# An RWKV block's first tile: both output shares from one difference, value and receptance projected the other way round, the second key in halves, and a second norm that takes no mean of its own

## The chip, the core and the metric

The kernel runs on one core of one Trainium2 chip. The metric is the device time of one execution in microseconds. Engines are called TensorE (PE in the profile, PEld for its weight loads), VectorE (DVE), ScalarE (ACT), GpSimd (POOL) and SyncE (SP, which only issues transfers here).

## What is computed

x has 2 sequences of 4096 steps with 256 features. Two residual blocks follow each other, each on a layer norm of its input (with no learned scale). The attention block mixes each step with the one before it, projects key, value and receptance, runs a recurrence along time, and projects back:

```python
xk = x * time_mix_k + x_prev * (1.0 - time_mix_k)
...
k = jnp.einsum('btd,ed->bte', xk, W_k)
v = jnp.einsum('btd,ed->bte', xv, W_v)
r = jax.nn.sigmoid(jnp.einsum('btd,ed->bte', xr, W_r))
...
new_p = jnp.maximum(p, u + k_t)
scale_old = jnp.exp(jnp.maximum(p - new_p, NEG_CLAMP))
scale_cur = jnp.exp(jnp.maximum(u + k_t - new_p, NEG_CLAMP))
wkv_t = (scale_old * q + scale_cur * v_t) / (scale_old + scale_cur + EPS)
new_p2 = jnp.maximum(p + w, k_t)
scale_prev = jnp.exp(jnp.maximum(p + w - new_p2, NEG_CLAMP))
scale_new = jnp.exp(jnp.maximum(k_t - new_p2, NEG_CLAMP))
q2 = scale_prev * q + scale_new * v_t
...
y = r * wkv
return jnp.einsum('btd,ed->bte', y, W_o)
```

The feed-forward block has two gates of 1024 (one through silu), two layers of 1024 x 1024 with gelu, and a layer back to 256; its weights are ternary, with a scale for each output.

## The kernel before

Features lie on partitions (two chunks of 128, ND = 2), time along the free axis in tiles of 512 steps (TS), 16 tiles in all. A tile goes through norm, attention, second norm and feed-forward. The feed-forward is the bulk: each fp32 operand is split into a rounded part (hi) and a rest (lo), and every product is taken with both (split_product, L185 and L186). While the feed-forward of tile i runs, the generators attention(i + 1) and normalise(i + 2) are stepped between its blocks, so their work lies under its matmuls. The loop at the end of split_block sets that order.

The first tile has nothing to lie under. It is written out by hand in first_tile. Its helpers matmul, activation, add and on chain every instruction behind the last one of its engine, so each engine works in the order of the text; all of them are recorded at L357. The order is:

- norm of tile 0 in two halves of 256 steps (first_layernorm): mean by a matmul with a matrix of 1/256, subtraction on VectorE, squares on ScalarE, their sum over the two chunks on VectorE, variance by matmul (var), root, reciprocal, spread over the partitions by matmul (rstd), product on VectorE.
- projections (project). Two ways are in use. One scales the weights by the mix and by one minus the mix (scale) and takes four matmuls, two on xn and two on xn shifted by a step: key and value. The other mixes xn first (mx, then: two ScalarE passes and a GpSimd add per chunk) and takes two matmuls: receptance.
- differences(h), scales(h), state(h), result(h) for the two chunks h: a scan along time for the log-maximum (lm), the clamped differences (sc for the state, so for the output), exponentials and sigmoids, a scan for the numerator (num), and the output y. The log-maximum and numerator after the last step are copied on GpSimd into log_max and numer; the second tile copies them into its own scan states on VectorE (L251, L252).
- the output projection into four banks of half a tile (ps_o), added to x_sb, and a second first_layernorm on the sum, with matmuls for its mean; then the split into x_hi and x_lo, with which the feed-forward starts.

keep_warm issues matmuls whose result is not read. load_table makes ScalarE load an activation table early. A small partition_all_reduce on root calls that GpSimd operation once ahead of its use. normalise(1) (called second) is stepped once near the end of first_tile: it issues the load of tile 2 on GpSimd's queue, adds the two chunks of tile 1 on VectorE (both, L204), and sums that over the partitions on GpSimd (total, L206).

Loads: x of tile 0 comes in halves on SP and ACT, the attention weights on ACT (key), SP (value, receptance) and GpSimd's queue (output). GpSimd's queue also carries x of tile 1, and then w1, w2 and h1 of the feed-forward.

Of the kernel before, what the change touches and what calls it, by code (L numbers as in the profile page):

```python
# [14 lines left out]
P = 128  # L15
# [51 lines left out]
def split_block(ctx, tc, flags, x, vecs, w_attn, w1, w2, h1, h2, w3, out):  # L67
# [35 lines left out]
    for m, queue in enumerate((nc.scalar, nc.sync, nc.sync)):  # L103
        queue.dma_start(out=wa_sb[:, m], in_=w_attn[:, m])
# [33 lines left out]
    vector.tensor_scalar(unmix, vec[:, 0 : 3 * ND], -1.0, 1.0, ALU.mult, ALU.add)  # L138

# [61 lines left out]
    def total(a, b, tag):  # L201

        both = one.tile([P, TS], F32, tag=tag, name="both")
        marks["both"] = vector.tensor_tensor(both, a, b, ALU.add)  # L204
        everywhere = one.tile([P, TS], F32, tag="total", name="total")
        marks["sum"] = nc.gpsimd.partition_all_reduce(everywhere, both, channels=P, reduce_op=ReduceOp.add)  # L206
        return everywhere

    def layernorm(src, new_xc, tag, spread=False):


        mean = total(src[:, 0, :], src[:, 1, :], tag)
        if spread:
            yield
        xc = new_xc()
        for h in range(ND):
            vector.scalar_tensor_tensor(xc[:, h, :], mean, -1.0 / D, src[:, h, :], ALU.mult, ALU.add)
        if not spread:
            yield
        sq = wide.tile([P, ND, TS], F32, tag="wide", name="sq")  # L220
        scalar.activation(sq, xc, AF.Square)
        var = total(sq[:, 0, :], sq[:, 1, :], tag)
        if spread:
            yield
        rstd = one.tile([P, TS], F32, tag=tag, name="rstd")
        scalar.activation(rstd, var, AF.Sqrt, bias=eps, scale=1.0 / D)  # L226
        if not spread:
            yield
        for p in halves:
            vector.reciprocal(rstd[:, p], rstd[:, p])  # L230
            if spread and p is halves[0]:
                yield
        for h in range(ND):
            vector.tensor_tensor(xc[:, h, :], xc[:, h, :], rstd, ALU.mult)
        yield
# [50 lines left out]
    def normalise(i):  # L286

        x_sb = loaded.pop(i)
        if i + 1 < len(tiles):
            loaded[i + 1] = load_x(i + 1)  # L290
        xn = []

        def new_xn():

            xn.append(one.tile([P, ND, TS + 1], F32, tag="xn", name="xn"))
            if tiles[i][1] == 0:
                vector.memset(xn[0][:, :, 0:1], 0.0)
            else:
                vector.tensor_copy(xn[0][:, :, 0:1], prev)
            return xn[0][:, :, 1:]  # L300

        yield from layernorm(x_sb, new_xn, "rstd1", spread=True)
        vector.tensor_copy(prev, xn[0][:, :, TS:])
        normal[i] = (x_sb, xn[0])
# [74 lines left out]
    def first_layernorm(src, xc, means):  # L379
# [4 lines left out]
        for mean, p in zip(means, halves):  # L384
            for h in range(ND):
                add(xc[:, h, p], src[:, h, p], mean, ALU.subtract)
            activation(sq[:, :, p], xc[:, :, p], AF.Square)
        varis = []
        for p in halves:
            add(sq[:, 0, p], sq[:, 0, p], sq[:, 1, p])  # L390
            var = ps_ffn.tile([P, TS // 2 // P], F32, tag="pf", name="var")
            for b in range(TS // 2 // P):
                t = slice(p.start + b * P, p.start + (b + 1) * P)
                matmul(var[:, b : b + 1], sq[:, 0, t], mean_w[:, 0:1], start=True, stop=True)
            varis.append(var)
            yield
# [12 lines left out]
        for rstd, p in zip(spread, halves):  # L409
            for h in range(ND):  # L410
                add(xc[:, h, p], xc[:, h, p], rstd, ALU.mult)
            yield

    def first_tile(second):

        x_sb = loaded.pop(0)
        xn = wide.tile([P, ND, TS], F32, tag="wide", name="xn0")
# [23 lines left out]
        norm = first_layernorm(x_sb, xn, means)  # L441
# [3 lines left out]
        scaled = [[hid.tile([P, ND, D], F32, tag=tag, name="ws") for tag in ("hi", "lo")] for m in range(2)]  # L445
# [5 lines left out]

        next(norm)
# [8 lines left out]
        keep_warm(unread, 3, 2 * P)  # L461
        scale(0, (1, 1), (0, 1))
        scale(1, (0, 0), (1, 0), (1, 1), (0, 1))
# [4 lines left out]
        for c in range(ND):  # L468
            j = 2 * ND + c
            activation(mx[:, c, :], xn[:, c, :], AF.Copy, scale=vec[:, j : j + 1])  # L470
            activation(then[:, c, 1:], xn[:, c, : TS - 1], AF.Copy, scale=unmix[:, j : j + 1])
            on("gpsimd", "tensor_tensor", mx[:, c, 1:], mx[:, c, 1:], then[:, c, 1:], ALU.add)
# [4 lines left out]

        def project(m, h, kind, p=whole):
# [3 lines left out]
            if m == 2:  # L482
                for c in range(ND):
                    matmul(ps, wa_sb[:, 2, c, block], mx[:, c, :], start=c == 0, stop=c == ND - 1)
                return ps
            now, then = (ws[:, :, block] for ws in scaled[m])
            skip = 1 if p.start == 0 else 0
            shifted = slice(p.start + skip - 1, p.stop - 1)
            matmul(ps, now[:, 0, :], xn[:, 0, p], start=True, stop=False)
# [6 lines left out]
        keys = [[(project(0, 0, attn, p), p) for p in halves], [(project(0, 1, attn), whole)]]  # L496
# [3 lines left out]
        def differences(h):  # L500
            w, u = col(DECAY, h), col(FIRST, h)
            for k, p in keys[h]:
                t, after = lm[h][:, p], lm[h][:, p.start + 1 : p.stop + 1]
                on("vector", "tensor_tensor_scan", after, w.to_broadcast([P, p.stop - p.start]), k,
                   lm[h][:, p.start : p.start + 1], ALU.add, ALU.max)
                on("vector", "scalar_tensor_tensor", sc[h][1][:, p], t, w, k, ALU.add, ALU.subtract)
                on("vector", "scalar_tensor_tensor", so[h][1][:, p], k, u, t, ALU.add, ALU.subtract)
# [3 lines left out]
        def scales(h):  # L511
            activation(sc[h][0], sc[h][0], AF.Exp)
            activation(sc[h][1], sc[h][1], AF.Relu)
            activation(sc[h][1], sc[h][1], AF.Exp, scale=-1.0)


        def state(h):
            on("vector", "scalar_tensor_tensor", sc[h][1], sc[h][1], MIN_SCALE, v[h], ALU.max, ALU.mult)
            on("vector", "tensor_tensor_scan", num[h][:, 1:], sc[h][0], sc[h][1], num[h][:, 0:1], ALU.mult, ALU.add)
            on("gpsimd", "tensor_copy", numer[:, h : h + 1], num[h][:, TS:])  # L520

        def result(h):
            for share, of in zip(so[h], (num[h][:, 0:TS], v[h])):
                on("vector", "scalar_tensor_tensor", share, share, MIN_SHARE, of, ALU.max, ALU.mult)
            add(so[h][0], so[h][0], so[h][1])

        for h in range(ND):
            differences(h)
            scales(h)
            activation(so[h][0], so[h][1], AF.Sigmoid, scale=-1.0)  # L530
            activation(so[h][1], so[h][1], AF.Sigmoid)
# [4 lines left out]
        state(0)  # L536
        result(0)
        state(1)
        add(y[:, 0, :], so[0][0], r[0], ALU.mult)
        result(1)  # L540
        for p in halves:
            add(y[:, 1, p], so[1][0][:, p], r[1][:, p], ALU.mult)
        with behind("vector"), behind("scalar"):
            next(second)
        last["vector"] = marks["both"]
# [3 lines left out]
        ]  # L549
        for c in range(ND):  # L550
            for ps_of, p in zip(banks, halves):
                for h in range(ND):
                    matmul(ps_of[h], wa_sb[:, 3, c, h * P : (h + 1) * P], y[:, c, p], start=c == 0, stop=c == ND - 1)
        means = []
        for ps_of, p in zip(banks, halves):
            mean = ps_ffn.tile([P, TS // 2], F32, tag="pf", name="mean")
            for h in range(ND):
                add(x_sb[:, h, p], x_sb[:, h, p], ps_of[h])
                matmul(mean, mean_w, x_sb[:, h, p], start=h == 0, stop=h == ND - 1)
            means.append(mean)  # L560
        unread = ps_attn.tile([P, TS], F32, tag="pa", name="unread")
        keep_warm(unread, 4)
        x2 = wide.tile([P, ND, TS], F32, tag="wide", name="x2")
        x2_hi = one.tile([P, ND, TS], F32R, tag="x2_hi", name="x2_hi")
        x2_lo = one.tile([P, ND, TS], F32R, tag="x2_lo", name="x2_lo")
        norm = first_layernorm(x_sb, x2, means)
        for _ in range(4):
            next(norm)
        keep_warm(unread, 6)
        run(norm)  # L570
        for p in halves:
            activation(x2_hi[:, :, p], x2[:, :, p], AF.Copy)
            add(x2_lo[:, :, p], x2[:, :, p], x2_hi[:, :, p].bitcast(F32), ALU.subtract)
# [8 lines left out]
    def ffn(i, x1, x2):  # L582

        ha = []
        for f in range(NH):
            fs = slice(f * P, (f + 1) * P)
            pa = ps_ffn.tile([P, TS], F32, tag="pf", name="pa")
            split_product(pa, lambda c: w1_sb[:, c, fs], x2)
            pb = ps_ffn.tile([P, TS], F32, tag="pf", name="pb")
            split_product(pb, lambda c: w2_sb[:, c, fs], x2)  # L590
# [55 lines left out]
    second = normalise(1)  # L646
    first_tile(second)
# [309 lines left out]
```

## Time and profile before

| what | us |
|---|---|
| runs of the kernel before | 1547.36, 1547.98, 1548.09 (median 1547.98) |
| the profiled execution | 1547.97 |
| its span, first to last instruction | 1546.2 |
| TensorE busy in the span | 1535.7 |
| VectorE, ScalarE, GpSimd busy | 1069.9, 1048.7, 241.2 |
| first feed-forward matmul starts | 39.91 |

In lines of the timeline and of the chain the first number is the start in us after the span's start, the second the length. Behind an instruction stands what it writes and reads (out<-in), its shape, and in brackets how long its engine was idle ahead of it and what ended the wait. TensorE's busy time is modelled, so its share says little; the start of one matmul against the start of the one before it says more. A 128x512 matmul in plain fp32 shows as two passes.

### The profile page before, as it was taken

What the parts mean: (1) busy time and instruction counts of PE and PEld (TensorE: products, weight loads), DVE (VectorE), ACT (ScalarE), POOL (GpSimd) and SP (SyncE); (2) the same over time, 40 slices, a digit from 0 to 9 for tenths busy, and PEclk for the clock granted to TensorE, in tenths of its full rate; (3) what the DMA queues carried; (4) which work ended last, traced back from release to release, by engine and by line L of the source; (5) the groups of instructions that cost most, each with busy time, mean ns of one, the idle gap of its engine ahead of it and who ended that gap; (6) DMA issues with size and microseconds to landing.
All of it is one profiled execution on the core that took longest, in us unless ns stands there. A gap on an engine that the chain in (4) does not pass through costs nothing.

```text
span 1546.2 us, 16526 instructions
## 1 busy us (share of the span) xinstructions
PE 1535.7 (99%) x6260; PEld 1173.5 (76%) x6260; DVE 1069.9 (69%) x1598; ACT 1048.7 (68%) x1349; POOL 241.2 (16%) x118
## 2 busy tenths in 40 slices
PE   9999999999999999999999999999999999999998
PEld 6778777777877778777787777877777787777886
DVE  6887676867768667785777767677685777855531
ACT  6685957759487595866858668595775858656542
POOL 4122012110211102112011121101111021100100
PEclk9999999999999999999999999999999999999999
DMA  7612031220302104031130311203122030210302
GB/s 266 142 43 101 14 116 35 70 81 14 130 22 95 55 17 141 7 109 41 42 116 9 120 35 54 97 9 121 35 75 75 14 130 21 96 41 29 115 9 82
DMA packets 39702, 109.16 MB, mean 71 GB/s; under 512 B 3712, under 2 KB 12672, under 8 KB 39104
## 3 DMA queue, kind: packets, MB, share of 16 engines
q1 hardware_dynamic: 25760, 79.86, 15.9%
q0 software_dynamic: 13296, 27.53, 5.8%
q8 instruction: 51, 0.84, 0.2%
q10 hardware_dynamic: 560, 0.66, 0.1%
q14 instruction: 35, 0.29, 0.1%
HBM read 99.64 MB, written 12.58 MB: 73 GB/s over the span
## 4 chain that ended last, share of the span: by engine, by line
PE 97%; DVE 2%; ACT 1%; issue 0%; DVEq 0%
PE ph L185 30%; PE ph L186 30%; PE pa L185 4%; PE po L186 4%; PE po L185 4%; PE pb L185 4%; PE pa L186 4%; PE pb L186 4%; PE ps_r L178 3%; PE ps_v L178 3%; PE ps_k L178 3%; PE ps_o L178 3%; PE ps_k L357 0%; PE unread L357 0%; DVE scale L357 0%
## 5 line engine op out<-in xcount | busy, mean ns | idle before, releaser
L185 PE MATMUL ph<-hi,h_sb 128*128 128x512 f32 x2048 | 818.1, 400 | 0.2 <-ACT hi L192 0.2
L186 PE MATMUL ph<-lo,h_sb 128*128 128x512 f32 x2048 | 812.3, 398 | 0.0
L185 PEld LDWEIGHTS ph<-hi,h_sb 128*128 128x128 f32 x2048 | 384.6, 188 | 100.0 <-issue 17.4
L186 PEld LDWEIGHTS ph<-lo,h_sb 128*128 128x128 f32 x2048 | 384.5, 188 | 99.1 <-issue 15.6
L206 POOL PARTITION_ALL_REDUCE total<-both x60 | 204.5, 3408 | 865.2 <-DVE both L204 424.4
L611 DVE TENSOR_TENSOR lo<-full,hi 128x512 fp32r<-128x512 f32 x256 | 195.8, 768 | 140.7 <-ACT full L610 137.3
L608 ACT ACTIVATE hi<-ph,vec 128x512 fp32r<-128x512 f32 x256 | 175.5, 685 | 126.6 <-PE ph L186 125.6
L592 ACT ACTIVATE gated<-pa,vec 128x512 f32<-128x512 f32 x128 | 87.3, 682 | 140.2 <-PE pa L186 138.4
L610 ACT ACTIVATE full<-ph,vec 128x512 f32<-128x512 f32 x256 | 174.9, 683 | 0.2
L593 DVE SCALAR_TENSOR_TENSOR gated<-pb,vec,gated 128x512 f32<-128x512 f32 x128 | 95.8, 749 | 71.0 <-PE pb L186 66.5
L608 ACT ACT_TABLE_LOAD x104 | 133.4, 1283 | 1.8
L230 DVE RECIPROCAL rstd<-rstd 128x256 f32<-128x256 f32 x60 | 102.6, 1729 | 2.6 <-ACT rstd L226 2.6
L192 ACT ACTIVATE hi<-gated 128x512 fp32r<-128x512 f32 x128 | 80.6, 630 | 35.1 <-DVE gated L593 34.8
L185 PE MATMUL pb<-x_hi,w_sb 128*128 128x512 f32 x256 | 102.0, 398 | 0.6 <-ACT gated L592 0.6
L185 PE MATMUL pa<-x_hi,w_sb 128*128 128x512 f32 x256 | 101.9, 398 | 0.1
L186 PE MATMUL pb<-x_lo,w_sb 128*128 128x512 f32 x256 | 100.6, 393 | 0.0
L186 PE MATMUL pa<-x_lo,w_sb 128*128 128x512 f32 x256 | 100.5, 393 | 0.0
L193 DVE TENSOR_TENSOR lo<-gated,hi 128x512 fp32r<-128x512 f32 x128 | 96.3, 761 | 5.8 <-ACT hi L192 0.7
L186 PE MATMUL po<-lo,w_sb 128*128 128x512 f32 x256 | 100.2, 392 | 0.0
L185 PE MATMUL po<-hi,w_sb 128*128 128x512 f32 x256 | 100.2, 391 | 0.0
L617 DVE SCALAR_TENSOR_TENSOR x_sb<-po,vec,x_sb 128x512 f32<-128x512 f32 x32 | 24.0, 751 | 73.4 <-PE po L186 73.4
L261 DVE TENSOR_TENSOR_SCAN lm<-vec,lm,ps_k 128x512 f32<-128x512 f32 x30 | 38.4, 1279 | 41.3 <-PE ps_k L178 41.3
(145 smaller groups left out, 1745.2 us busy)
## 6 DMA issues: line engine op xcount, KB each, us to landing
h_sb<-h_hbm SPq DMA_DIRECT2D x128, 512.0 KB, 3.3
raw<-in_h SPq DMA_DIRECT2D x32, 256.0 KB, 2.7
x_sb<-in_x POOLq DMA_DIRECT2D x15, 512.0 KB, 4.0
out<-x_sb POOLq DMA_DIRECT2D x15, 512.0 KB, 3.1
h_sb<-in_h POOLq DMA_DIRECT2D x1, 4096.0 KB, 20.1
h_hbm<-in_h POOLq DMA_DIRECT2D x8, 512.0 KB, 8.9
w_sb<-in_w POOLq DMA_DIRECT2D x3, 1024.0 KB, 10.9
raw<-in_w SPq DMA_DIRECT2D x12, 256.0 KB, 2.6
```

The lines of the kernel that those rows point to most:

```text
L178: tensor.matmul(psum, weights(c), src[c], start=c == 0, stop=c == n - 1)
L185: tensor.matmul(psum, weights(c), hi, start=c == 0, stop=False)
L186: tensor.matmul(psum, weights(c), lo, start=False, stop=c == n - 1)
L192: marks["rounded"] = scalar.activation(hi, full, AF.Copy)
L193: marks["rest"] = vector.tensor_tensor(lo, full, hi.bitcast(F32), ALU.subtract)
L206: marks["sum"] = nc.gpsimd.partition_all_reduce(everywhere, both, channels=P, reduce_op=ReduceOp.add)
L230: vector.reciprocal(rstd[:, p], rstd[:, p])
L592: scalar.activation(full, pa, AF.Silu, scale=col(S1, f))
L593: vector.scalar_tensor_tensor(full, pb, col(S2, f), full, ALU.mult, ALU.mult)
L608: scalar.activation(hi, ps, AF.Gelu, scale=col(scales, f))
L610: marks["rounded"] = scalar.activation(full, ps, AF.Gelu, scale=col(scales, f))
L611: marks["rest"] = vector.tensor_tensor(lo, full, hi.bitcast(F32), ALU.subtract)
```

## The change

Everything is in the first tile and in the first block of its feed-forward.

- The output shares are no longer computed from a difference of their own. The difference for the state, p + w - k (sc[h][1]), plus or minus a constant per feature (offset, decay plus first), gives both sigmoids' arguments through the bias of the activation. One VectorE pass per half key goes, and sigmoids of both chunks follow each other (shares), after the exponentials of both.
- Value is projected from mixed inputs (mx), with 2 matmuls for each chunk; receptance from one chunk with scaled weights and one mixed chunk (mxr), with 3. The receptance weights are loaded ahead of the value weights.
- The key of the second chunk is projected and scanned in halves, as that of the first was.
- state(1) stands ahead of result(0).
- The second norm takes no mean: the output weights are centred (each row of them less its own mean over the outputs), the first norm's centred input xc is kept apart from xn (in the buffer of x2_lo), and xc plus the product with the centred weights is the centred sum. The product with the plain weights is computed too (gain, 4 matmuls of 512 columns) and added to x_sb later, for the residual. The variance matmuls sum over both chunks, and the VectorE sum of squares goes from the second norm (not from the first).
- The sum of the two chunks of tile 1 (both) moves from VectorE to GpSimd, near the start of first_tile.
- keep_warm in the second norm: 2 in place of 4, and gain[1] in place of 6. The split is taken chunk by chunk for the rest, and the first feed-forward block takes all products with the rounded part first.

```diff
-    for m, queue in enumerate((nc.scalar, nc.sync, nc.sync)):
+    for m, queue in ((0, nc.scalar), (2, nc.sync), (1, nc.sync)):
         queue.dma_start(out=wa_sb[:, m], in_=w_attn[:, m])
...
+    offset = const.tile([P, 2, ND], F32, name="offset")
+    vector.tensor_tensor(offset[:, 0, :], vec[:, DECAY : DECAY + ND], vec[:, FIRST : FIRST + ND], ALU.add)
+    vector.tensor_scalar(offset[:, 1, :], offset[:, 0, :], -1.0, None, ALU.mult)
...
-    def first_layernorm(src, xc, means):
+    def first_layernorm(xc, out, centre):
         sq = wide.tile([P, ND, TS], F32, tag="wide", name="sq")
-        for mean, p in zip(means, halves):
-            for h in range(ND):
-                add(xc[:, h, p], src[:, h, p], mean, ALU.subtract)
-            activation(sq[:, :, p], xc[:, :, p], AF.Square)
         varis = []
         for p in halves:
-            add(sq[:, 0, p], sq[:, 0, p], sq[:, 1, p])
+            centre(xc, sq, p)
+        yield
+        for p in halves:
             var = ps_ffn.tile([P, TS // 2 // P], F32, tag="pf", name="var")
+            chunks = range(1 if xc is not out else ND)
+            if xc is not out:
+                add(sq[:, 0, p], sq[:, 0, p], sq[:, 1, p])
             for b in range(TS // 2 // P):
                 t = slice(p.start + b * P, p.start + (b + 1) * P)
-                matmul(var[:, b : b + 1], sq[:, 0, t], mean_w[:, 0:1], start=True, stop=True)
+                for c in chunks:
+                    matmul(
+                        var[:, b : b + 1], sq[:, c, t], mean_w[:, 0:1], start=c == 0, stop=c == chunks[-1]
+                    )
...
+        with behind("vector"):
+            on("gpsimd", "tensor_tensor", summed, loaded[1][:, 0, :], loaded[1][:, 1, :], ALU.add)
         scale(0, (1, 1), (0, 1))
-        scale(1, (0, 0), (1, 0), (1, 1), (0, 1))
+        scale(2, (0, 1), (1, 1))
         run(norm)
         mx, then = (wide.tile([P, ND, TS], F32, tag="wide", name="mx") for _ in range(2))
-        for c in range(ND):
-            j = 2 * ND + c
-            activation(mx[:, c, :], xn[:, c, :], AF.Copy, scale=vec[:, j : j + 1])
-            activation(then[:, c, 1:], xn[:, c, : TS - 1], AF.Copy, scale=unmix[:, j : j + 1])
-            on("gpsimd", "tensor_tensor", mx[:, c, 1:], mx[:, c, 1:], then[:, c, 1:], ALU.add)
+        mxr, thenr = (hid.tile([P, TS], F32, tag=tag, name="mxr") for tag in ("hi", "lo"))
+        for m, c, mixed, step in ((1, 0, mx[:, 0, :], then[:, 0, :]), (1, 1, mx[:, 1, :], then[:, 1, :]), (2, 0, mxr, thenr)):
+            j = m * ND + c
+            activation(mixed, xn[:, c, :], AF.Copy, scale=vec[:, j : j + 1])
+            activation(step[:, 1:], xn[:, c, : TS - 1], AF.Copy, scale=unmix[:, j : j + 1])
+            on("gpsimd", "tensor_tensor", mixed[:, 1:], mixed[:, 1:], step[:, 1:], ALU.add)
...
+        centred = hid.tile([P, ND, D], F32, tag="hi", name="centred")
+        row = tmp.tile([P, ND], F32, tag="each", name="row")
+        for c in range(ND):
+            on("vector", "tensor_reduce", row[:, c : c + 1], wa_sb[:, 3, c, :], mybir.AxisListType.X, ALU.add)
+        on("vector", "tensor_scalar", row, row, 1.0 / D, None, ALU.mult)
+
+        def centre(c):
+            on("vector", "tensor_scalar", centred[:, c, :], wa_sb[:, 3, c, :], row[:, c : c + 1], None, ALU.subtract)
+
+        centre(0)
...
-            if m == 2:
+            if m == 1:
                 for c in range(ND):
-                    matmul(ps, wa_sb[:, 2, c, block], mx[:, c, :], start=c == 0, stop=c == ND - 1)
+                    matmul(ps, wa_sb[:, m, c, block], mx[:, c, :], start=c == 0, stop=c == ND - 1)
                 return ps
...
+            if m == 2:
+                matmul(ps, now[:, 1, :], xn[:, 1, :], start=True, stop=False)
+                matmul(ps[:, 1:], then[:, 1, :], xn[:, 1, shifted], start=False, stop=False)
+                matmul(ps, wa_sb[:, m, 0, block], mxr, start=False, stop=True)
+                return ps
...
-        keys = [[(project(0, 0, attn, p), p) for p in halves], [(project(0, 1, attn), whole)]]
+        keys = [[(project(0, h, attn, p), p) for p in halves] for h in range(ND)]
...
-                on("vector", "scalar_tensor_tensor", so[h][1][:, p], k, u, t, ALU.add, ALU.subtract)
...
         def scales(h):
+            activation(so[h][0], sc[h][1], AF.Relu)
+            activation(so[h][0], so[h][0], AF.Exp, scale=-1.0)
             activation(sc[h][0], sc[h][0], AF.Exp)
-            activation(sc[h][1], sc[h][1], AF.Relu)
-            activation(sc[h][1], sc[h][1], AF.Exp, scale=-1.0)
+        def shares(h):
+            activation(so[h][1], sc[h][1], AF.Sigmoid, bias=offset[:, 1, h : h + 1])
+            activation(sc[h][1], sc[h][1], AF.Sigmoid, bias=offset[:, 0, h : h + 1], scale=-1.0)
...
-        for h in range(ND):
-            differences(h)
-            scales(h)
-            activation(so[h][0], so[h][1], AF.Sigmoid, scale=-1.0)
-            activation(so[h][1], so[h][1], AF.Sigmoid)
+        differences(0)
+        scales(0)
+        differences(1, lambda: centre(1))
+        scales(1)
+        for h in range(ND):
+            shares(h)
...
         state(0)
+        state(1)
         result(0)
-        state(1)
...
+        gain = [ps_sum.tile([P, TS], F32, tag="ps", name="gain")]
+        def output(h, c):
+            matmul(gain[h], wa_sb[:, 3, c, h * P : (h + 1) * P], y[:, c, :], start=c == 0, stop=c == ND - 1)
         for c in range(ND):
             for ps_of, p in zip(banks, halves):
                 for h in range(ND):
-                    matmul(ps_of[h], wa_sb[:, 3, c, h * P : (h + 1) * P], y[:, c, p], start=c == 0, stop=c == ND - 1)
-        means = []
-        for ps_of, p in zip(banks, halves):
-            mean = ps_ffn.tile([P, TS // 2], F32, tag="pf", name="mean")
-            for h in range(ND):
-                add(x_sb[:, h, p], x_sb[:, h, p], ps_of[h])
-                matmul(mean, mean_w, x_sb[:, h, p], start=h == 0, stop=h == ND - 1)
-            means.append(mean)
-        unread = ps_attn.tile([P, TS], F32, tag="pa", name="unread")
-        keep_warm(unread, 4)
+                    matmul(ps_of[h], centred[:, c, h * P : (h + 1) * P], y[:, c, p], start=c == 0, stop=c == ND - 1)
+            output(0, c)
+        unread = ps_attn.tile([P, TS], F32, tag="pa", name="unread")
+        gain.append(ps_attn.tile([P, TS], F32, tag="pa", name="gain"))
+        keep_warm(unread, 2)
+        def plus_output(x2, sq, p):
+            for h in range(ND):
+                add(x2[:, h, p], xc[:, h, p], banks[p.start * 2 // TS][h])
+                activation(sq[:, h, p], x2[:, h, p], AF.Square)
...
-        keep_warm(unread, 6)
+        for c in range(ND):
+            output(1, c)
         run(norm)
...
+        for h in range(ND):
+            add(x_sb[:, h, :], x_sb[:, h, :], gain[h])
...
+            if i + f:
+                split_product(pa, lambda c: w1_sb[:, c, fs], x2)
+                split_product(pb, lambda c: w2_sb[:, c, fs], x2)
+            else:
+                for k in range(2):
+                    for ps, sb in ((pa, w1_sb), (pb, w2_sb)):
+                        for c in range(ND):
+                            tensor.matmul(
+                                ps, sb[:, c, fs], x2[c][k], start=k + c == 0, stop=k == 1 and c == ND - 1
+                            )
```

## The prediction

> **What bounds the kernel now.** I read the page first. The chain that ended last is TensorE for all but 3% of the span:
>
> ```profile
> span 1546.2 us, 16526 instructions
> ...
> PE 97%; DVE 2%; ACT 1%; issue 0%; DVEq 0%
> ```
>
> The tiles after the first keep TensorE fed and the change leaves their order as it was, so only the way to the first feed-forward matmul can move the time. That way is short. The chain of waits in order of time, cut to 10 to 42 us (start, length, what):
>
> ```profile
> 11.29 6.88 PE ps_k L357 x24
> 18.17 3.44 PE ps_v L357 x8
> ...
> 21.72 0.70 DVE scale L357
> ...
> 22.44 1.30 DVE state L357
> ...
> 28.35 1.21 DVE scale L357 x2
> ...
> 30.85 1.99 PE ps_o L357 x8
> 32.84 1.74 PE mean L357 x8
> ...
> 35.39 0.64 ACT sq L357
> ...
> 36.54 0.61 PE var L357 x4
> ...
> 39.91 0.50 PE pa L185
> ```
>
> Three stretches: TensorE projects until the first value is there (21.6), VectorE works without a gap from 21.72 to the first half of y[1] (30.38 + 0.42 = 30.80), and then projection, mean, norm and split run one after another until the feed-forward starts at **39.91**. Every microsecond off 39.91 is one off the end, as far as the backlog of the first feed-forward allows. The profiled execution took 1547.97 us with a span of 1546.2, so 1.8 lie around it; the median of the three runs is 1547.98, and I sum against 1547.97.
>
> Last I read the timeline of GpSimd, because the change gives it work (start, length, what, in brackets the idle time before):
>
> ```profile
> 16.03 0.20 POOL L357 COPY prev<-xn 128x2 f32<-128x2 f32 x1
> 23.93 0.86 POOL L357 PARTITION_ALL_REDUCE root<-eps  x1 [7.70 <-ACT scale L357]
> ...
> 27.95 0.90 POOL L96 DMA_DIRECT2D x_sb<-in_x  x1
> ...
> 31.83 3.26 POOL L206 PARTITION_ALL_REDUCE total<-both  x1 [2.12 <-DVE both L204]
> ...
> 49.31 3.23 POOL L206 PARTITION_ALL_REDUCE total<-both  x1 [8.59 <-DVE both L204]
> ```
>
> and beside the last of these VectorE:
>
> ```profile
> 49.03 0.74 DVE L593 SCALAR_TENSOR_TENSOR gated<-pb,vec,gated 128x512 f32<-128x512 f32 x1
> 49.86 2.22 DVE L193 TENSOR_TENSOR lo<-gated,hi 128x512 fp32r<-128x512 f32 x1
> ```
>
> Two facts. The first all-reduce (on root) comes 7.70 us after the copy of prev, though it needs only an activation that was done at 16.24: its first use costs 7.7. And a VectorE operation with two SBUF inputs that starts during an all-reduce ends 2.78 us after the all-reduce began (49.31 to 52.08; the next at 97.79 does the same to an add, 98.25 + 2.32 = 100.57). Operations with one input in PSUM pass: during the one at 31.83 the four adds of ps_o take 0.42 each as always.
>
> **Part by part.**
>
> *Projections.* A 128x512 matmul is two passes of 0.43 (24 passes of ps_k, half of them 256 wide, 11.13 to 18.0). Value goes from 8 matmuls to 4 (16 passes to 8), receptance from 4 to 6. The first value is ready at 18.0 + 4 x 0.43 + 0.16 = 19.9 instead of 21.6; receptance ends 4 passes, 1.7, earlier, at 26.8. The second key in halves costs no pass and gives its first scan at 16.5. ScalarE trades two weight scalings (0.40 apart) for two more mixings (0.61 apart): its last mixing starts at 14.5 instead of 14.0. The value weights now load behind the receptance weights (the two SP loads take 7.4 to landing, issued by 2.6): both are there by some 10.3, needed at 10.6 and 18. Nothing.
>
> *Shares from one difference.* One VectorE pass of 0.48 fewer for each half key (three passes, with the full one of 0.75), two table loads of 1.28 fewer on ScalarE, two one-input passes more. VectorE gets two row sums, a small scaling and a centring of 128x256 ahead of the first scan. None is in the trace; bounds from 0.17 (128x6) to 0.75 (scan of 256), I take 0.42 (a 128x256 add) and 0.30, in all 1.3 after xn ends at 11.73, so 13.0 against the key at 13.06: hidden; if it is 1.3 late, the gap before the second key (16.5) takes half of it. The differences end at 20.1. State(0) could start at 20.1, not 21.72: **-1.6, if nothing else is late.**
>
> *What is late next.* The second tile's sum (both) now runs on GpSimd early, so its all-reduce waits no longer for VectorE, and it starts as soon as GpSimd's queue lets it: mixings (three, 1.28 each, the last at 15.3), copy of prev at 16.5, 7.70 for the first use, 24.4; 0.74 later four copies at 0.125, done by 25.75; the load of tile 2 with 0.90, and the all-reduce at **26.6 to 29.9**, amid the y chain. Two prices. (a) VectorE's copies of log_max and numer into the next tile's state (L251, L252) stand in its order ahead of the add of result(0), and wait for GpSimd's copies until 25.7; VectorE comes there at 25.2. Behind them: add, y[0], result(1), y[1], and TensorE's ps_o. (b) Add 25.8 to 26.5, y[0] to 27.1, then share x numerator of h = 1, two SBUF inputs, meets the all-reduce: it ends at 26.6 + 2.78 = 29.4 instead of 27.8. Then 0.6 (share x v), 0.69 + 0.04 (add), y[1] first half 30.74 to **31.16**. Before: 30.80. The gain of the first stretch is gone: **+0.36**. Bounds for (b): 0 (all-reduce elsewhere) to 2.2.
>
> [...]
>
> *The sum on GpSimd itself.* Tile 1 lands at 1.30 + 6.6 = 7.9 (DMA view), so both (1.28, as the mixing of 511) runs at about 8.1 to 9.4, where VectorE adds the squares of the second half (8.37 to 8.79, two SBUF inputs). No row shows a GpSimd add against such an operation. Bounds: 0, or to the end of it, 9.4 + 0.42, which moves var from 9.09 to 9.88: +0.8 for all behind it. The nearest row is the all-reduce, which blocks for two thirds of its length: **+0.5**.
>
> *Second norm.* From y[1] on TensorE is a queue without holes: 8 passes ps_o 8 x 0.215 = 1.72, gain[0] 2 x 0.43 = 0.86, two warmers 2 x 0.235 = 0.47, a switch of 0.11, var of both chunks 16 x 0.115 = 1.84 (before: 4 loads in 0.52 for half of one half's work), rstd to the start of gain[1] 1.19, gain[1] 4 x 0.43 = 1.72: 7.9. Squares (ends 34.1), roots, products (end 38.4) and x_hi (second chunk 39.2) fit within it, the last just. Before it was 30.85 to 39.91 = 9.06; gone are mean (8 passes), subtraction (1.6) and sum of squares (0.43). **-1.1.** Gained outputs are added to x_sb by VectorE (2 x 0.68) before the first gated product is due: nothing, at most 0.7.
>
> *First feed-forward block.* pa is complete after its sixth matmul and not its eighth, some 0.25 sooner after the start. TensorE later idles there 1.2 us behind VectorE and ScalarE (pb at 51.69 to 52.92) and 0.8 at 61; I take **-0.25**, bounds 0 and -0.5.
>
> Sum: +0.36 + 0.5 - 1.1 - 0.25 = -0.5. **Forecast 1547.4.**
>
> **Rivals.**
>
> 1. *The all-reduce misses the y chain* (first use shorter or longer, so that the VectorE operations lie beside it in another order). Then y[1] follows VectorE alone: 29.2; TensorE is free at 26.9 + 1.72 + 0.86 = 29.5; feed-forward at 29.5 + 7.9 = 37.4, -2.5, and -0.25: **1545.2**. Against: 3.3 us of blocking in a chain of 9 us whose operations are two-SBUF for half of the time.
> 2. *Both blocks at full price* (+0.8 instead of +0.5, and no gain in the backlog): +0.36 + 0.8 - 1.1 = 0: **1548.0**. The change would do what it says and gain nothing.
> 3. *Slower: TensorE loses its rate.* The first matmuls of the program take 0.43 for 512 columns of the short kind (eight in 3.78), those of the feed-forward 0.23; the change drops six of ten warmers and leaves TensorE idle from 29.5 to 31.2. If that idle time lowers the rate, some 5 us (as at the start, 1.3 to 6.3) run at half: 5 x (1 - 0.23/0.43) = +2.3, **1549.7**. It decides if an idle of 1.7 us is enough; against it, after the idle 51.92 to 52.92 the next matmuls are 0.23 apart again.
>
> **How the numbers follow.** Forecast 0.50, rival 1 0.20, rival 2 0.19, rival 3 0.07, other 0.04 (half each way). The range leaves out most of rival 3 and the lower edge of rival 1: 1544.9 to 1549.0. A difference of 0.2%, 3.1 us, is about what a measurement of this kernel can tell from no change: faster means below 1544.9, a third of rival 1 and the odd case, 0.08; slower above 1551.1, 0.04; the rest, 0.88, is the same.
>
> **What would show it.** In the profile after: the all-reduce on total at 26 to 28, with a two-SBUF product or add of 2 us beside it; y[1] at 31 (rival 1: at 29.2); the add of squares at 8.4 stretched to 1 us or not; TensorE without a hole from y[1] to the feed-forward in 7.9 us; first pa at 39.2 to 39.7. Wrong would be: a first feed-forward before 38, or matmuls of the feed-forward 0.43 apart.

## The result, and the profile after

The changed kernel takes 1558.12 us (median of 6 runs, 1557.65 to 1558.96) against 1547.78 for the kernel before (median of 6, 1547.36 to 1548.09): 1.0067 times as long, interval 1.0057 to 1.0077. It is 10.3 us slower, and far outside the range. The profiled execution took 1557.65, with a span of 1555.9. The page of the kernel after, its span and its chain:

```profile
span 1555.9 us, 16540 instructions
...
PE 98%; DVE 1%; ACT 0%; issue 0%; POOL 0%; DVEq 0%
```

The chain is even more TensorE's than before (97%), so the time did not go into a new wait. The first tile went much as predicted. GpSimd's timeline of the kernel after:

```profile
8.78 1.32 POOL L362 TENSOR_TENSOR both<-x_sb 128x512 f32<-128x512 f32 x1 [3.81 <-DMA x_sb<-in_x]
...
24.95 0.40 POOL L362 PARTITION_ALL_REDUCE root<-eps  x1 [8.01 <-ACT scale L362]
...
26.68 3.20 POOL L211 PARTITION_ALL_REDUCE total<-both  x1
```

VectorE's timeline beside the last of these:

```profile
25.83 0.68 DVE L362 TENSOR_TENSOR scale<-scale 128x512 f32<-128x512 f32 x1
26.62 0.69 DVE L362 TENSOR_TENSOR y<-scale,ps_r 128x512 f32<-128x512 f32 x1
27.22 2.19 DVE L362 SCALAR_TENSOR_TENSOR scale<-scale,state 128x512 f32<-128x512 f32 x1
...
31.25 0.75 DVE L362 TENSOR_TENSOR y<-scale,ps_r 128x256 f32<-128x256 f32 x2 [0.52 <-DVE scale L362]
```

and TensorE's behind that:

```profile
31.73 1.99 PE L362 MATMUL ps_o<-y,centred 128*128 128x256 f32 x8 [1.51 <-DVE y L362]
...
37.82 1.88 PE L362 MATMUL gain<-y,wa_sb 128*128 128x512 f32 x4
39.14 1.03 PE L650 MATMUL pa<-x_hi,w_sb 128*128 128x512 f32 x2
```

The all-reduce falls into the chain to y[1] (26.68), a product with two SBUF inputs beside it takes 2.19, and the first feed-forward matmul still starts 0.77 sooner than before. What happens to that lead, from the starts of the first matmuls of each stage in both traces:

| start of | before | after | difference |
|---|---|---|---|
| first feed-forward matmul | 39.91 | 39.14 | -0.77 |
| its first hidden layer (ph) | 55.82 | 55.60 | -0.21 |
| feed-forward of the second tile | 136.27 | 136.22 | -0.04 |
| output layer (po) of the third tile | 317.81 | 318.82 | +1.02 |
| output layer of the last tile | 1531.65 | 1540.86 | +9.21 |
| end of the span | 1546.19 | 1555.87 | +9.68 |

**The loss lies in the tiles that the change does not touch**, 0.6 to 0.7 us in each. The order of the instructions is the same there. The pace is not. In the view of one tile's instructions the numbers are the shortest, median and longest duration in ns; in the traces of both kernels a duration is the start-to-start distance of back-to-back matmuls plus 162 (389 at a distance of 227). The first hidden layer of the third tile, the second, and po; the kernel before:

```profile
L185 PE MATMUL ph<-hi,h_sb x39: 388/392/792, 247.0 to 274.7; 128*128 128x512 f32 x39
L185 PE MATMUL ph<-hi,h_sb x55: 387/389/791, 285.7 to 313.7; 128*128 128x512 f32 x55
L185 PE MATMUL po<-hi,w_sb x16: 388/392/394, 317.8 to 324.7; 128*128 128x512 f32 x16
```

The kernel after:

```profile
L189 PE MATMUL ph<-hi,h_sb x39: 392/394/797, 247.0 to 274.7; 128*128 128x512 f32 x39
L189 PE MATMUL ph<-hi,h_sb x55: 387/389/793, 285.8 to 313.8; 128*128 128x512 f32 x55
L189 PE MATMUL po<-hi,w_sb x16: 392/394/399, 318.8 to 325.8; 128*128 128x512 f32 x16
```

The second hidden layer keeps its 389. The first and po take some 4 ns more for each matmul: the fastest now are as slow as the median was. At the same granted clock (0.999), 4.4 ns (means below) for 2048 + 512 matmuls are 11 us.

What differs for these matmuls is where their operands lie. The change allocates a constant of 16 bytes, offset, ahead of prev, and in the built kernels everything behind it, the activations hi and lo among it, starts 32 bytes later (prev at 83424 before and at 83456 after), while w1, w2, h1 and w3 in front stay. The profile shows no addresses; these are the ones in the built kernels. Addresses in a partition, as remainders of 512 (h2_sb holds the weights of the second hidden layer, which are streamed in):

```
                 w1 w2 h1 w3   hi, lo   streamed h2_sb   x2_hi  x2_lo
before                   384      448              448     320    320
after                    384      480              480     352    288
```

### The profile page after: what moved, and what is told of

Same layout as the page of the kernel before. It is cut to its first block, busy times and chain, and to the rows that moved or that the text cites. A ratio compares the mean times of both kernels' runs of the same rounds, so it can differ in the third digit from the quotient of the medians.

```text
span 1555.9 us, 16540 instructions
## 1 busy us (share of the span) xinstructions
PE 1544.2 (99%) x6264; PEld 1173.7 (75%) x6264; DVE 1071.1 (69%) x1599; ACT 1046.9 (67%) x1350; POOL 243.2 (16%) x120
## 4 chain that ended last, share of the span: by engine, by line
PE 98%; DVE 1%; ACT 0%; issue 0%; POOL 0%; DVEq 0%
PE ph L189 30%; PE ph L190 30%; PE pb L189 4%; PE po L190 4%; PE po L189 4%; PE pa L189 4%; PE pa L190 4%; PE pb L190 4%; PE ps_o L182 3%; PE ps_r L182 3%; PE ps_v L182 3%; PE ps_k L182 3%; PE unread L362 0%; DVE scale L362 0%; ACT scale L362 0%; PE ps_k L362 0%
## 5 line engine op out<-in xcount | busy, mean ns | idle before, releaser
L190 PEld LDWEIGHTS ph<-lo,h_sb 128*128 128x128 f32 x2048 | 384.4, 188 | 103.7 <-issue 14.9
```

The lines of the kernel that those rows point to most:

```text
L190: tensor.matmul(psum, weights(c), lo, start=False, stop=c == n - 1)
```

## The experiments

| kernel | us, median (runs) | ratio to before, interval |
|---|---|---|
| before_shift32 | 1559.25 (4) | 1.0073 [1.0056, 1.0090] |
| before_hid32 | 1558.75 (4) | 1.0069 [1.0052, 1.0086] |
| before_minus64 | 1543.49 (7) | 0.9971 [0.9959, 0.9982] |
| after_unshifted | 1548.79 (10) | 1.0005 [0.9996, 1.0015] |
| before_weights64 | 1543.82 (7) | 0.9974 [0.9963, 0.9985] |
| before_h2_32 | 1559.23 (4) | 1.0073 [1.0057, 1.0088] |
| before_aligned | 1536.86 (4) | 0.9927 [0.9912, 0.9942] |
| before_spread | 1555.98 (4) | 1.0052 [1.0037, 1.0067] |
| after_apart | 1546.63 (11) | 0.9992 [0.9983, 1.0001] |
| after_tie1 | 1550.92 (11) | 1.0017 [1.0008, 1.0026] |
| after_best | 1535.41 (5) | 0.9921 [0.9908, 0.9935] |
| after_best2 | 1533.02 (4) | 0.9904 [0.9889, 0.9919] |

The kernel before took 1547.86 to 1548.06 beside them.

### Is it the place, or the changed first tile?

**before_shift32**: nothing of the change but 32 bytes.

```diff
+    pad = const.tile([P, 8], F32, name="pad")
+    vector.memset(pad, 0.0)
     prev = const.tile([P, ND, 1], F32, name="prev")
```

> The kernel before with one unread constant of 32 bytes put where the change puts its own new constant, so that every tile allocated behind it starts 32 bytes later; no instruction but the one that fills it is added. Theory A (placement: TensorE reads the hidden activations, which moved by 32 bytes, more slowly): about 9 to 11 us over the kernel before, some 1558, and the feed-forward matmuls on ph 231 ns apart in the median where the kernel before has 227. Theory B (the other rotation of the shared buffers, which the changed first tile causes) and theory C (the changed first tile leaves something behind that slows all later tiles, such as a queue or a table): no difference, 1547.8 within 1.

Measured 1559.25, 11.3 more. The whole loss comes with 32 unread bytes; B and C fall.

**before_hid32** puts the same 32 bytes into a pool of their own just ahead of the pool hid.

> The kernel before with 32 unread bytes right ahead of the pool of the hidden activations: these and the streamed weights behind them move by 32 bytes, all other tiles stay. Theory A in its narrow form (it is what TensorE reads in the three hidden layers): 9 to 11 us slower, some 1558, as with all tiles moved. Theory A in its wide form (the tiles of VectorE, ScalarE or the DMAs slow the others down): less than half of that, under 1552. Theories B and C: no difference.

Measured 1558.75. Moving hi, lo and the streamed weights alone does it; with x, x2 and the tiles of the attention block moved along (before_shift32) it was 1559.25, so where those lie accounts for some 0.5 of this loss at most. The first hidden layer of its third tile:

```profile
L187 PE MATMUL ph<-hi,h_sb x39: 392/394/798, 247.0 to 269.9; 128*128 128x512 f32 x39
```

**before_minus64** puts eps and unmix into one tile, and log_max and numer into another, which frees 64 bytes.

> The kernel before with four small constants in two tiles instead of four, so that every tile allocated behind them starts 64 bytes earlier. If it is the place within a block of 64 bytes that counts: no difference, 1547.8 within 1. If it is any other place than the one before (a conflict between two tiles whose distance or absolute address matters): it moves, by up to some 10 us, in either direction.

Measured 1543.49: 4.4 faster than the kernel before. Its ph and po are 227 ns apart throughout. So blocks of 64 bytes are not the rule, and the kernel before was itself not at the best place.

**after_unshifted**: the changed kernel, offset in the 16 bytes that pad rounded.

```diff
-    rounded = const.tile([P, len(pieces)], F32, name="rounded")
+    kept_offset = const.tile([P, len(pieces) + 4], F32, name="rounded")
+    rounded = kept_offset[:, : len(pieces)]
+    offset = kept_offset[:, len(pieces) :].rearrange("p (a b) -> p a b", b=ND)
```

> The changed kernel with its new constant put into 16 bytes that were padding of another, so that all later pools start where they start in the kernel before; the computation and the order of the work stay. Theory A: the ten microseconds go away and only the first tile's difference is left, -0.2 to -0.8, so 1547.0 to 1547.6. Theories B and C: it stays at 1558.

Measured 1548.79. Nine of the ten microseconds go. But the first tile is worse than in the kernel after, by more than the expectation allows: first feed-forward matmul at 40.30. VectorE's and then GpSimd's timeline of this kernel show why:

```profile
8.26 1.43 DVE L362 TENSOR_TENSOR sq<-sq 128x256 f32<-128x256 f32 x1 [0.24 <-ACT sq L362]
```

```profile
8.13 1.27 POOL L362 TENSOR_TENSOR both<-x_sb 128x512 f32<-128x512 f32 x1 [3.16 <-DMA x_sb<-in_x]
```

In the kernel after VectorE's line is this:

```profile
8.54 0.43 DVE L362 TENSOR_TENSOR sq<-sq 128x256 f32<-128x256 f32 x1 [0.36 <-ACT sq L362]
```

GpSimd's wait for the load of tile 1 ended at 8.13 here and at 8.78 in the kernel after. Here GpSimd's sum began first, and the sum of squares is stretched from 0.43 to 1.43; there VectorE had begun (8.54) before GpSimd (8.78) and kept its 0.43. In these two profiles the prediction's block came with the earlier landing and not with the later one.

### What about the place?

The second hidden layer gave the lead: the 32 bytes of pad moved its activations and its streamed weights together, and it never left 227 ns. That made theory D, the distance between the two operands of a matmul.

**before_weights64** moves the weights and leaves the activations.

```diff
+    prev = const.tile([P, ND, 1], F32, name="prev")
+    log_max = const.tile([P, ND], F32, name="log_max")
     w1_sb = const.tile([P, ND, HID], F32R, name="w1_sb")
...
-    prev = const.tile([P, ND, 1], F32, name="prev")
-    log_max = const.tile([P, ND], F32, name="log_max")
```

> The kernel before with two small constants (prev, log_max) allocated ahead of the four feed-forward weights instead of behind them: the weights move by 64 bytes, and every tile from x_sb on, the hidden activations among them, stays where it is. Theory D (what counts is the distance between the streamed operand and the weights of the same matmul, as remainders of 512 bytes; the kernel before has 64 of it in the first hidden layer and the output layer, 0 in the second hidden layer, whose matmuls are 227 ns apart without exception): the distance becomes 0 there too, the matmuls on ph and po come to 227 ns throughout, and the time to 1543.5 within 0.7, as with all later tiles 64 bytes earlier. Theory E (the absolute place of the activations counts): they didn't move, so no difference, 1547.9 within 0.7.

Measured 1543.82, as D has it. Its po is even to the nanosecond:

```profile
L185 PE MATMUL po<-hi,w_sb x16: 389/389/389, 316.7 to 323.5; 128*128 128x512 f32 x16
```

**before_h2_32** does the reverse: 32 bytes between hid and the pool of the streamed weights.

> The kernel before with 32 unread bytes between the hidden activations and the streamed weights of the second hidden layer: only these weights (and the raw pieces behind them) move. Theory D: the distance of the second hidden layer goes from 0 to -32, its 2048 matmuls leave their 227 ns for some 229 to 232, and the time goes up by 4 to 10 us, to 1552 to 1558; the first hidden layer and po stay as they are. Theory E (place of the activations): no difference, 1547.9 within 0.7.

Measured 1559.23, a little beyond the range given. The first hidden layer stays at 392, the second leaves its 389 for the first time:

```profile
L187 PE MATMUL ph<-hi,h_sb x41: 388/392/792, 246.7 to 274.9; 128*128 128x512 f32 x41
L187 PE MATMUL ph<-hi,h_sb x54: 388/395/795, 285.8 to 313.9; 128*128 128x512 f32 x54
```

**before_aligned** brings x2 to the weights' remainder too: the odd-sized tiles (each, xn, lm, num) go ahead of x2 and the small constants are joined as in before_minus64. No work is added or taken out.

```diff
+    few = ctx.enter_context(tc.tile_pool(name="few", bufs=3))
     one = ctx.enter_context(tc.tile_pool(name="one", bufs=1))
...
+    one.tile([P, ND, TS + 1], F32, tag="xn", name="xn")
+    for tag in ("lm", "num"):
+        one.tile([P, TS + 1], F32, tag=tag, name=tag)
...
-            each = tmp.tile([P, TS // 2 // P], F32, tag="each", name="each")
+            each = few.tile([P, TS // 2 // P], F32, tag="each", name="each")
```

> The kernel before with the same work and the same tiles in other places: the hidden activations, the two halves of the normalised input x2 and the weights all at the same remainder of 512 bytes (before: 64 and -64 apart). Theory D: ph and po at 227 ns as with 64 bytes less, and pa and pb, of which a pair of matmuls takes 466 ns in every kernel so far, come down to 454 for the pair, 6 ns for each of 1024 matmuls, 6.1 us: 1547.9 - 4.4 - 6.1 = 1537.4 within 1. Theory D without the input layer (its matmuls are slow for another reason, such as the shape of x2): 1543.5 within 0.7.

Measured 1536.86, 11.0 faster than before, with the same instructions. The input layer, the kernel before first:

```profile
L185 PE MATMUL pa<-x_hi,w_sb x16: 393/398/398, 325.1 to 338.7; 128*128 128x512 f32 x16
L186 PE MATMUL pa<-x_lo,w_sb x16: 388/393/393, 325.4 to 338.9; 128*128 128x512 f32 x16
```

and before_aligned:

```profile
L186 PE MATMUL pa<-x_hi,w_sb x16: 389/389/389, 323.6 to 336.8; 128*128 128x512 f32 x16
L187 PE MATMUL pa<-x_lo,w_sb x16: 389/389/389, 323.9 to 337.0; 128*128 128x512 f32 x16
```

**before_spread** puts the weights in the order w3, w2, w1, h1 with the small constants between them, for distances that no kernel had.

> The kernel before with the weights in another order and the small constants between them, so that the distances to the streamed operand (remainders of 512 bytes) are: w3 32, w2 256, h1 192, w1 64; activations, x2 and the streamed weights stay. Theory D with a period of 512: only the second hidden layer stays at 227 ns; h1, w1 and w2 run 3 to 6 ns slower than that, w3 at 228 to 231, and the time is 1550 to 1558. Theory D with a period of 256 or less: pb (w2) runs at 227 ns. If a small positive distance is cheaper than a far one (64 gave 229, 96 some 232 in the kernels so far): po at 227 to 229, h1 at 232 or more.

Measured 1555.98, within the range; po, at 233.3, is slower than the 228 to 231 that theory D was given for it. No distance but 0 gives 227 in the mean, 256 (pb, 229.0) included, so the period is not 256 or less. It is at most 512: po's sixteen blocks of w3 lie 512 bytes apart, and all take 389 in before_weights64. "A small positive distance is cheap" falls: 32 (233.3) is as dear as any. From all traces, the mean start-to-start distance of these matmuls without a hole, from 240 us on:

| operand less weights, remainder of 512 | ns | where |
|---|---|---|
| 0 | 226.7 to 227.6 | every layer, in the kernels that have it there |
| 64 | 229.0; 230.5 | h1 and po in before; pa in before_spread |
| 256 | 229.0 | pb in before_spread |
| 32 | 233.3 | po in before_spread |
| 96 | 233.4 | h1 and po in after, before_shift32, before_hid32 |
| 192 | 233.4 | h1 in before_spread |
| -32, -64, -128 | 233.0 to 233.5 | h2 in before_h2_32; pa and pb in before; in before_minus64 |
| -32 and -96 in turn | 231.7 | pa and pb in after (x2_hi, x2_lo) |

A distance of 64 has two paces, so the distance sets most of the pace and not all of it. With this table the result adds up. After less before: 2048 matmuls on h1 x 4.4 = 9.0, 512 on po x 4.4 = 2.3, and 1024 on pa and pb x -1.4 (233.2 to 231.75, x2 at -32 and -96) = -1.4. From the second tile's feed-forward to the last tile's po there are 15/16 of the first and last and 14/16 of the middle one: 9.1, against 9.25 measured (1404.64 less 1395.38).

### What the first tile's two blocks are worth

**after_apart** is after_unshifted with two ties on GpSimd, one-column copies that wait for VectorE.

```diff
         with behind("vector"):
+            on("gpsimd", "tensor_copy", summed[:, 0:1], squares[0][:, 0, TS - 1 :])
             on("gpsimd", "tensor_tensor", summed, loaded[1][:, 0, :], loaded[1][:, 1, :], ALU.add)
...
+        tie = tmp.tile([P, ND], F32, tag="each", name="tie")
+        on("gpsimd", "tensor_copy", tie[:, 0:1], y[:, 1, TS // 2 - 1 : TS // 2])
```

> The changed kernel with its later tiles where the kernel before has them, and two ties on GpSimd: its sum of the second tile waits for VectorE's last sum of squares (in the profile without the tie it ran beside it and stretched it from 0.43 to 1.43 us), and the all-reduce of that sum waits for the first half of y[1] (without the tie it ran through the chain to y[1] and stretched a product to 2.19 us). If these two blocks cost what the first tile lost: y[1] first half at 29.2 to 29.6, first feed-forward matmul at 37.4 to 37.9, 1545.2 to 1545.7. If one of them hides nothing (another wait ends last behind it): first feed-forward matmul at 38.5 to 39.2, 1546.3 to 1547.2.

Measured 1546.63, between the two cases; first feed-forward matmul at 37.95. y[1] now starts at 30.05, not 29.2: VectorE waits for GpSimd's copies instead, which stand behind its first all-reduce (at 25.25, 8.56 after the copy of prev), and TensorE is busy with y[0] until then:

```profile
25.82 0.15 DVE L256 COPY lm<-log_max 128x1 f32<-128x1 f32 x1 [0.78 <-POOL log_max L362]
```

**after_tie1** keeps the first tie alone.

> The changed kernel with its later tiles where the kernel before has them, and only the first of the two ties of after_apart: GpSimd's sum of the second tile waits for VectorE's last sum of squares. It splits the 2.2 us between after_unshifted (1548.8) and after_apart (1546.6) by their cause. If the stretched sum of squares (1.43 us in place of 0.43) passes through to the first feed-forward matmul: 1547.8 within 0.4, and the all-reduce amid the chain to y[1] is worth the other 1.1. If the all-reduce hides it (VectorE waits there for GpSimd's copies in any case): 1548.3 to 1548.8, and the tie of the all-reduce is worth 1.7 to 2.2 by itself.

Measured 1550.92, and spread wide (1547.96 to 1552.91): neither case, worse than no tie at all. With this tie GpSimd issues the load of tile 2 early (8.76), so the all-reduce comes at 25.52 (in the kernel after at 26.68, with that load just ahead of it at 25.72), just ahead of the sum that leads to y[0]. VectorE's line of that sum, then TensorE's:

```profile
25.59 2.77 DVE L362 TENSOR_TENSOR scale<-scale 128x512 f32<-128x512 f32 x1
```

```profile
29.21 3.13 PE L362 MATMUL ps_o<-y,centred 128*128 128x256 f32 x8 [2.65 <-DVE y L362]
32.13 1.62 PE L362 MATMUL gain<-y,wa_sb 128*128 128x512 f32 x2
```

The same eight matmuls take 2.00 elsewhere, the two of gain 1.02. The view by windows (us, TensorE busy, granted clock, transfers) of this kernel tells why:

```profile
29.00:29.50 0.50, 0.29 (x1) 1.00 0.00 0
29.50:30.00 0.50, 0.50 (x4) 0.91 0.00 0
30.00:30.50 0.50, 0.50 (x3) 0.50 0.13 24
...
32.50:33.00 0.50, 0.50 (x2) 0.50 1.41 261
33.00:33.50 0.50, 0.50 (x2) 0.68 1.56 272
```

That is the prediction's third rival, alive in a variant: an idle of 2.65 us is followed by some 3.4 us at a granted clock of 0.50, which begin at 29.9, 0.7 after the matmuls had started again. In the kernel after the idle was 1.51 and the clock stayed at 1.00. Over the whole span the granted clock is 0.999 in the two fastest of the eleven (1547.96 and 1548.11) and 0.998 or 0.997 in the others; the kernel before has 0.998 in some runs too, so whether the slower clock came in every execution was not shown.

### A version that beats both

**after_best** joins after_apart and the places of before_aligned.

> The changed kernel with both repairs: the two ties on GpSimd, and hidden activations, x2 and weights all at the same remainder of 512 bytes. If the two are independent, their gains add up: after_apart (1546.6) less what the places gave the kernel before (1547.9 - 1536.9 = 11.0), so 1535.6 within 0.7, 1.2 below the kernel before in the same places. If a faster feed-forward in the first tile waits for the other engines (its first blocks already wait for VectorE and ScalarE), some of it is lost: up to 1536.9.

Measured 1535.41: the two add up.

**after_best2** also moves the first all-reduce behind the copies.

```diff
-        on("gpsimd", "partition_all_reduce", root, eps, channels=P, reduce_op=ReduceOp.add)
...
         state(1)
+        on("gpsimd", "partition_all_reduce", root, eps, channels=P, reduce_op=ReduceOp.add)
```

> As after_best, but GpSimd copies the states of the first tile before its first all-reduce (on root) and not behind it. In after_apart VectorE waited 0.78 us for these copies (24.97 to 25.82), ahead of the sum that leads to y[0]. If that wait was the one that ended last: y[0] and all behind it 0.6 to 0.8 earlier, 1534.8 to 1535.0. If another wait takes its place (y[1] behind the gate of the second half, the roots of the second norm): no difference to after_best. If the first use of the all-reduce, now about 24.3 to 32, makes the second tile's mean late: slower than after_best.

Measured 1533.02, below the range given: 14.9 less than the kernel before and 3.8 less than the kernel before in the same places. The chain of waits from the key's projection on is TensorE's alone:

```profile
11.07 6.90 PE ps_k L366 x32
17.98 3.43 PE ps_v L366 x8
21.41 5.15 PE ps_r L366 x12
26.56 0.04 issue
26.60 1.99 PE ps_o L366 x8
28.59 0.86 PE gain L366 x2
```

The profiled executions of the two kernels differ by 2.0 (spans of 1533.2 and 1531.2), and only 0.48 of it lies there (first feed-forward matmul 37.34 to 36.88, and 0.48 at each stage from the third tile on). The other 1.5 lies at the end: 13.19 us from the first po matmul of the last tile to the end of the span, where all other kernels have 14.5 to 15.0. All of it comes after the last addition to x_sb, which ends 5.0 us before the end of the span here and 6.5 in after_best. What shortened the program's end was not tried, so I do not count it to the copies.

## Why the prediction was wrong

**The step that failed** is "The tiles after the first keep TensorE fed and the change leaves their order as it was, so only the way to the first feed-forward matmul can move the time." The first half is true, and the conclusion does not follow: the order was kept, the addresses were not. 32 bytes in a list of constants changed the pace of 2560 matmuls, for +9.25 us between the second tile's feed-forward and the last tile's po, 90% of the loss. No rival held this, so the range could not. It was to be seen ahead: the kernel before shows 392 in the first hidden layer and 389 in the second for the same shape, and I did not ask why.

The terms of the first tile, each by its own size (their sum of -0.5 from 1547.97 gives 1547.5, where the forecast says 1547.4):

- *First stretch, +0.36*: +0.87 (y[1], first half, ends at 31.67 against 30.80). The mechanism held: all-reduce 26.68 (26.6), sum from 25.83 (25.8), product ended 29.41 (29.4). The 0.5 more is an idle of VectorE ahead of y[1], 0.52 here and 0.52 in after_apart and after_tie1 too; its cause is open. The first use of the all-reduce, taken at 7.70, took 8.01 here, 8.56 in after_apart and only 5.66 in after_best2, where it comes later; why is open too.
- *The sum on GpSimd itself, +0.5*: 0 in this profile, and 1.0 in that of after_unshifted. I had taken a middle; in these two it is one or the other, with GpSimd's sum starting at 8.78 or, released earlier by its load, at 8.13.
- *Second norm, -1.1*: -1.65 (31.73 to 39.14, 7.41, against 9.06). TensorE had no hole, as said.
- *First feed-forward block, -0.25*: +0.56, from the lead of 0.77 to 0.21 at the first ph. TensorE waits there for ScalarE's gated (0.6 ahead of pb before, 1.0 after), so some 0.4 of the earlier start went into a longer wait.

Together the first tile gave -0.04 by the second tile's feed-forward (the lead of 0.21 shrinks on the way there), where I had -0.5: near rival 2, "The change would do what it says and gain nothing". Rival 1 was built as after_apart: the first feed-forward matmul came at 37.95 for 37.4, since VectorE then waits for GpSimd's copies, and with that wait gone too, in after_best2, at 36.88.

The prediction took from the rows of the all-reduce that a VectorE operation with two SBUF inputs is held for two thirds of GpSimd's time. The all-reduce did the same again: in the kernel after the product ended at 29.41, less its own 0.68 is 28.73, 2.05 after the all-reduce had begun (26.68) and 1.15 before it ended. The plain GpSimd sum held longer: in after_unshifted the stretched sum of squares ended at 9.69, less its own 0.43 is 9.26, 1.13 after GpSimd's sum had begun (8.13) and 0.14 before it ended (9.40).

## What to carry to other kernels

When an edit adds or resizes a tile, compare the addresses of all tiles behind it, not only the order of instructions. For streams of matmuls like these (fp32r, 512 columns, weights loaded for each), put the streamed operand and its weights at the same remainder of 512 bytes: pad, reorder or join small tiles until they are (here 227 ns for each, where other distances took 229 to 233.5), and read the durations of one layer for evenness (389/389/389) as the test. And two identical layers that run at different paces are a question to settle before any forecast.

## What was not expected of the hardware

- The distance of a matmul's two operands costs 0 or 2 to 7 ns of some 230, with nothing else changed (227 to 233.5 in the table). In the plain fp32 projections of the later tiles a pass of 512 columns takes 428.5 to 429.2 ns before and after, though their operands lie 32 bytes farther on from their weights; no kernel had them at distance 0, so whether 0 would help there was not tried. The profile shows weight loads (PEld) beside the matmuls, busy for 1173.5 of the 1546.2 us in the kernel before; why the distance of the two operands counts, no run shows. Moving the attention block's tiles, x and x2 along made 0.5 us (1559.25 with them, 1558.75 without), and moving the weights alone, by 64 bytes to distance 0, gave 1543.82. Why 64 and 256 (229.0 to 230.5) are cheaper than 32 and 96 (233.3, 233.4) stays open.
- An idle of 2.65 us was followed by 3.4 us at a granted clock of 0.50 (after_tie1); one of 1.51 was not (the kernel after).
- A GpSimd sum of 128x512 held a VectorE operation with two SBUF inputs until 1.13 of its 1.27 us had passed (after_unshifted), an all-reduce of 3.2 us until 2.05 had (the kernel after). Where VectorE's operation had begun first, it was not stretched (0.43, in the kernel after). The spans of GpSimd in a profile are rough.
